# A conditioned transformer block on one core: gate rows in four column groups, order rules for 13 of 64 attention steps, and MLP differences behind the split of the maxima

## Chip, cores and metric

The kernel runs on one core of a Trainium2 chip. The metric is device time in microseconds (us), the median of several executions. One execution was also taken with the hardware profiler.

## What is computed

x is (8, 1024, 512) float32, the condition is (8, 512), with 16 heads of width 32 and an MLP of width 2048. The reference, cut to what matters:

```python
mod = silu(condition) @ Wada + bada
sh_a, sc_a, gt_a, sh_m, sc_m, gt_m = split(mod, 6, axis=1)
xm = layernorm(x, g1, be1) * (1 + sc_a[:, None]) + sh_a[:, None]
x = x + gt_a[:, None] * (causal_attention(xm, Wqkv) @ Wproj + bproj)
xm = layernorm(x, g2, be2) * (1 + sc_m[:, None]) + sh_m[:, None]
h = gelu(xm @ W1 + b1)            # the exact form
x = x + gt_m[:, None] * (h @ W2 + b2)
```

## The kernel before

The 8 x 1024 rows are 16 blocks n of 512 rows: batch n // 2, half h = n % 2. A block of the second half attends to both halves of its batch. Its 16 heads are four groups g of four heads. An attention step is a pair (n, g); there are 64.

**Attention, twice over.** First come the scores of a group (`scores_at_once`, tiles sc_n_g_..., L1791): query tokens by keys, for four heads at once by four row groups of 32. VectorE adds the mask on the diagonal (L1805) and takes row maxima (L1808). `split_maxima` writes each maximum as a sum of three bfloat16 numbers into the tile mcols by four small operations (L1827 to L1830), on GpSimd or VectorE. TensorE turns them into a row (L1846), ScalarE copies that to mrow (L1852). Then `weights_T` computes the transposed scores (tiles st_n_g_k): TensorE first writes the negative maxima (L1872) and then adds the scores (L1884), ScalarE takes the exponent into a tile pT (L1897), GpSimd masks the diagonal (L1902) and sums the tiles pT (L2010). `weigh` multiplies with the values (tile po, L1925), `finish` sums over keys by a matmul with ones (L1946) and normalizes. The tiles sc and st share one place in PSUM, four banks large; po has one; three single banks serve all else.

**Linear work.** All projections and the MLP go through `strassen` and `down`, seven half-size products in place of eight; every product is 16 or 64 matmuls with 128 contraction rows, 32 output rows and 256 columns (`matmul`, L233), four beside each other in four column groups. Products A11 and A12 of a step go into one bank; A12 may start only when the copy p1 of A11 (p_proj for the output projection, L214) is out. In `down`, the second MLP matrix, VectorE and GpSimd make differences of hidden tiles hT (`combine`, L1378) between the products: after the product B22 of part 1 and its sum v3, VectorE replaces B22 by B22 − B12, and two more combinations follow. `settle` multiplies a result by its gate row and adds it to the residual rows xr. Weights arrive through a ring of nine tiles w_0, w_1, ... filled by SyncE's queue.

**Turned rows.** For most blocks the normalized rows are transposed by VectorE in 32 x 32 squares (L817), written to DRAM in four pieces (L830) and read back in four pieces (L836) to become xm_a or xm_m, the input of the projections and of the MLP.

**What sets the order.** While it writes the program, the kernel keeps its own estimate of each engine's time (`now`, `note`, `note_pe`). Linear work runs in threads; `step_aside`, ahead of every attention piece, lets linear work go first until its planned share is done or until the attention piece would wait less than the linear work. Small elementwise operations go through `either`, which takes VectorE only if it would end 1000 ns (`margin`) earlier than GpSimd. Transfers wait in a list (`transfers`) until the queue has room.

**Gate rows.** `gates(kind)` multiplies the activated condition (condT, 8 columns of a 32-column group) with the two gate parts of Wada: for each of four contraction tiles and two halves one matmul of 8 output rows and 256 columns (L582). VectorE adds bada (L222), and for the attention's gate also multiplies bproj by it (L591). The rows of 8 batches go to DRAM in one write each (L596), and `gate_broadcasts` reads one of them into 128 partitions per batch (L602).

## Time and profile before

| | us |
|---|---|
| median of 3 runs | 3461.78 |
| lowest and highest | 3461.54 and 3462.37 |
| the profiled execution | 3463.39 |
| its span | 3461.7 |

| engine | busy us | share | instructions |
|---|---|---|---|
| TensorE matmuls (PE) | 3420.8 | 99% | 55538 |
| weight loads (PEld) | 1775.8 | 51% | 55538 |
| VectorE (DVE) | 2068.1 | 60% | 2304 |
| ScalarE (ACT) | 1289.5 | 37% | 1424 |
| GpSimd (POOL) | 1939.0 | 56% | 2092 |

The granted clock of TensorE is 1.00 in the whole span. In the rows of the profile a line such as L233 is a line of the kernel before; "out<-in" are the tiles written and read, without their numbers, then the shape and the count. A row of the timeline begins with its start and its length in us; what stands in square brackets is idle time of that engine just before and what ended it. A float32 matmul of the program is two instructions in the trace, and matmuls that run beside each other overlap, so busy times of single matmuls don't add up.

### The profile page before, as it was taken

The numbers are of one execution on the slowest core, as the hardware profiler recorded it, in microseconds if no ns is written. First come the engines' busy times: TensorE is split into PE (matmuls) and PEld (weight loads), VectorE is DVE, ScalarE is ACT, GpSimd is POOL, SyncE is SP. The second block draws the span as 40 slices with busy tenths as digits, with TensorE's granted clock in tenths as the row PEclk, the third lists the DMA queues.
The fourth block names the chain that finished last, engine by engine and source line by source line (L and its number), as shares of the span: only waits on it lengthen the run. The fifth ranks groups of instructions, "written<-read, shape, count | busy, mean of one in ns | idle before, by whom it ended". The sixth has DMA issues, their size and how long they took to land.

```text
span 3461.7 us, 122760 instructions
## 1 busy us (share of the span) xinstructions
PE 3420.8 (99%) x55538; PEld 1775.8 (51%) x55538; DVE 2068.1 (60%) x2304; ACT 1289.5 (37%) x1424; POOL 1939.0 (56%) x2092
## 2 busy tenths in 40 slices
PE   8999999999999999999999999999999999999999
PEld 5544554455544554455554455454554545545555
DVE  6765666646566465664657546575466755556454
ACT  2345244343243433434333352433524334242431
POOL 3666757756267472774626755277553775446520
PEclk9999999999999999999999999999999999999999
DMA  7832434345544455444544445444464444633344
GB/s 230 277 124 87 122 113 130 103 126 150 172 136 129 128 151 159 135 139 130 162 145 136 136 133 169 138 134 136 132 177 134 130 146 122 192 110 102 117 144 136
DMA packets 380429, 490.71 MB, mean 142 GB/s; under 512 B 28436, under 2 KB 236364, under 8 KB 379908
## 3 DMA queue, kind: packets, MB, share of 16 engines
q1 hardware_dynamic: 379712, 482.59, 46.4%
q8 instruction: 437, 7.16, 0.8%
q14 instruction: 84, 0.69, 0.1%
q10 hardware_dynamic: 196, 0.28, 0.0%
HBM read 429.22 MB, written 53.53 MB: 139 GB/s over the span
## 4 chain that ended last, share of the span: by engine, by line
PE 89%; DVE 4%; DMA 3%; ACT 2%; issue 1%; POOL 1%; SPq 0%; DVEq 0%; ACTq 0%; POOLq 0%
PE bank L233 61%; PE sc L1791 8%; PE po L1925 7%; PE st L1884 7%; PE st L1872 3%; DVE mx L1808 2%; PE bank L1946 2%; DMA w<-kept_up_S 1%; ACT pT L1897 1%; DMA xm_m<-turned_m 1%; DVE sc L1805 1%; PE bank L1846 1%; DVE hT L1378 0%; ACT hT L1309 0%; PE bank L887 0%
## 5 line engine op out<-in xcount | busy, mean ns | idle before, releaser
L2010 POOL TENSOR_TENSOR pT<-pT,pT 128x256 f32<-128x256 f32 (+3 forms) x1254 | 1218.8, 1007 | 159.6 <-ACT pT L1897 121.9
L1897 ACT ACTIVATE pT<-st 128x2048 f32<-128x2048 f32 x288 | 541.1, 1879 | 1007.8 <-PE st L1884 892.6
L233 PE MATMUL bank<-w,hT 128*32 128x256 f32 x14336 | 814.4, 380 | 0.0
L1808 DVE TENSOR_REDUCE mx<-sc 128x4 f32<-128x2048 f32 (+3 forms) x384 | 665.5, 1754 | 196.3 <-PE sc L1791 190.2
L233 PEld LDWEIGHTS bank<-w,hT 128*32 128x32 f32 x14336 | 453.8, 110 | 357.8 <-issue 74.2
L233 PE MATMUL bank<-xm_m,w 128*32 128x256 f32 x8192 | 499.2, 380 | 1.5 <-issue 1.0
L233 PE MATMUL bank<-t_m,w 128*32 128x256 f32 x6144 | 383.8, 380 | 0.8 <-DMA w<-kept_up_S 0.4
L1902 POOL TENSOR_SCALAR_AFFINE_SELECT pT<-pT 128x512 f32<-128x512 f32 x256 | 181.0, 725 | 359.0 <-ACT pT L1897 357.3
L233 PEld LDWEIGHTS bank<-xm_m,w 128*32 128x32 f32 x8192 | 255.5, 110 | 229.9 <-issue 64.3
L1791 PE MATMUL sc<-kT,qT 32*128 32x512 f32 (+3 forms) x3072 | 329.1, 520 | 3.2 <-DVE mx L1808 3.0
L1805 DVE TENSOR_TENSOR sc<-sc,mask 128x1024 f32<-128x1024 f32 (+1 forms) x160 | 162.7, 1017 | 250.5 <-PE sc L1791 174.0
L1925 PE MATMUL po<-pT,v 128*32 128x512 f32 (+3 forms) x3072 | 304.8, 491 | 0.0
L1884 PE MATMUL st<-qT,kT 32*128 32x512 f32 (+3 forms) x3072 | 300.0, 486 | 0.0
L233 PEld LDWEIGHTS bank<-t_m,w 128*32 128x32 f32 x6144 | 189.9, 110 | 177.3 <-issue 53.1
L233 PE MATMUL bank<-xm_a,w 128*32 128x256 f32 x3968 | 239.5, 380 | 1.8 <-ACT xm_a L902 1.1
L190 POOL TENSOR_TENSOR qT<-top,rec 128x512 f32<-128x512 f32 x59 | 77.3, 1310 | 280.5 <-ACT rec L1964 277.5
L222 DVE TENSOR_TENSOR hT<-bank,u_u 128x512 f32<-128x512 f32 x192 | 130.1, 686 | 150.4 <-PE bank L233 147.4
L1791 PEld LDWEIGHTS sc<-kT,qT 32*128 32x128 f32 x3072 | 129.4, 183 | 159.7 <-issue 58.0
L233 PE MATMUL bank<-w,qT 128*32 128x256 f32 (+1 forms) x3008 | 188.9, 389 | 2.3 <-DVE p_proj L214 2.3
L233 PE MATMUL bank<-t_a,w 128*32 128x256 f32 x2944 | 179.4, 380 | 0.0
L233 PEld LDWEIGHTS bank<-xm_a,w 128*32 128x32 f32 x3968 | 126.7, 110 | 98.0 <-issue 16.1
L1309 ACT ACTIVATE hT<-hT,cols 128x512 f32<-128x512 f32 x256 | 164.1, 711 | 23.1 <-DVE hT L222 22.4
(246 smaller groups left out, 3414.8 us busy)
## 6 DMA issues: line engine op xcount, KB each, us to landing
w<-in_L_cond_W_dram SPq DMA_DIRECT2D x384, 256.0 KB
w<-kept_up_S SPq DMA_DIRECT2D x256, 256.0 KB
w<-kept_down_S SPq DMA_DIRECT2D x256, 256.0 KB
w<-kept_qkv_S SPq DMA_DIRECT2D x180, 256.0 KB
w<-in_L_cond_Wqkv_dram SPq DMA_DIRECT2D x147, 256.0 KB
hat<-in_x_dram SPq DMA_DIRECT2D x64, 256.0 KB
xr<-in_x_dram SPq DMA_DIRECT2D x64, 256.0 KB
out_dram<-xr SPq DMA_DIRECT2D x64, 256.0 KB
```

The source lines that it names most:

```text
L222: nc.vector.tensor_tensor(out, src, other, op)
L233: nc.tensor.matmul(ps[r], columns, rhs, start=start, stop=stop, skip_group_check=True)
L1309: nc.scalar.activation(hT[:, i, :], hT[:, i, :], AF.Gelu, bias=cols[:, O_B1 + f : O_B1 + f + 1])
L1791: nc.tensor.matmul(sc[:, j, c0 : c0 + w], qTs[n][r, gg, ts(qt, P)], keys_of(n, kh)[r, gg, :w], start=True, stop=True, skip_group_check=True,)
L1805: nc.vector.tensor_tensor(place, place, shape_of.to_broadcast(place.shape), ALU.add)
L1808: nc.vector.tensor_reduce(maxima[n, gg][:, kh, qt, :], sc[:, :, c0 : c0 + w], axis=AX.X, op=ALU.max)
L1872: nc.tensor.matmul(st[:, j, c0 : c0 + w], minus_ones[r, :], row[r, TB - w :], start=(c0 == 0), stop=False, skip_group_check=True,)
L1884: nc.tensor.matmul(st[:, j, c0 : c0 + w], kT[r, gg, ts(k % NTT, P)], qT[r, gg, TB - w :], start=False, stop=True, skip_group_check=True,)
L1897: nc.scalar.activation(pT[:, :, :used], st[:, :, :used], AF.Exp, scale=scale)
L1902: nc.gpsimd.affine_select(diagonal, diagonal, pattern=[[0, HPG], [1, P]], compare_op=ALU.is_ge, fill=0.0, base=0, channel_multiplier=-1,)
L1925: nc.tensor.matmul(po[r, TB - w :], v[:, k % NTT, g * P + j * hd : g * P + (j + 1) * hd], pT[:, j, c0 : c0 + w], start=(k == 0), stop=last ...
L2010: nc.gpsimd.tensor_tensor(into, into, pT[:, j, c0 : c0 + w], ALU.add)
```

## The change

**Gates.** Each contraction tile now meets four column groups of 128 columns, with all 32 columns of condT, so that the four quarters of a gate row stand below each other in one bank. The bias rows bada and bproj are loaded as one row each and spread over the groups by a matmul with ones. VectorE copies the result and, for the attention, multiplies the spread bproj by it. Each row then goes to DRAM in four writes of 8 x 128, which wait in the list of transfers.

**Order rules.** A table MANNER gives 13 attention steps their own `margin` and a value `leaning`, all others (1000, 0). A leaning of 300 lets an attention piece go first although linear work could start up to 200 ns earlier, or although it waits 300 ns itself. In `settle`, block 0 has margin 0.

**Behind the split.** After v3, VectorE makes a copy of one column of mcols, if the split in progress is about to end; the MLP differences stand behind that copy in VectorE's queue.

```diff
-    def either(out, a, b, op, reads, writes):
+    def either(out, a, b, op, reads, writes, slack=None):
...
-        if max(now["DVE"], t) + on_dve + margin[0] < max(now["POOL"], t) + on_pool:
+        if max(now["DVE"], t) + on_dve + (margin[0] if slack is None else slack) < max(now["POOL"], t) + on_pool:
...
-    costs = {"at": 16 * TR, "mt": 16 * TR, "gates": 4 * MM, "mod": 4 * MM}
+    costs = {"at": 16 * TR, "mt": 16 * TR, "gates": 2 * MM, "mod": 4 * MM}
...
-        ps = banks[bank][:B, :]
-        for fh in range(2):
-            for k in range(NC):
-                if fh + k:
-                    yield [], []
+        def spread_rows(r, start, stop):
+            for j in range(HPG):
                 nc.tensor.matmul(
-                    ps[:, half(fh, HB)], condT[:, k, :B], part[k // 2, fh][:, k % 2, :],
-                    start=fh + k == 0, stop=k == NC - 1, skip_group_check=True,
+                    banks[bank][j * hd : (j + 1) * hd, ts(r, P)], ones[:1, :hd], rows[r][:, ts(j, P)],
+                    start=start, stop=stop, skip_group_check=True,
                 )
-                note_pe(2 * COLUMN * HB, "columns", [], [("l", bank)])
-        release(*at)
-        combine_out(b_gate, bank, ps, b_gate)
+            note_pe(2 * COLUMN * P, "columns", [], [("l", bank)])
+        for k in range(NC):
+            for j in range(HPG):
+                nc.tensor.matmul(
+                    banks[bank][j * hd : (j + 1) * hd, :P], condT[:, k, :],
+                    part[k // 2, j // 2][:, k % 2, ts(j % 2, P)],
+                    start=k == 0, stop=False, skip_group_check=True,
+                )
+            note_pe(2 * COLUMN * P, "columns", [], [("l", bank)])
+            yield [], []
+        release(*at)
+        for r in range(len(rows)):
+            spread_rows(r, r > 0, True)
+        made = tmp.tile([P, TB], F32, tag="y", name=f"gates_{kind}")
+        gate = made[:, :P]
+        nc.vector.tensor_copy(gate, banks[bank][:, :P])
...
+                    nc.sync.dma_start(there[:, ts(j, P)], made[j * hd : j * hd + B, ts(r, P)])
...
+    def behind_split():
+        if rows_due and now["DVE"] < due([("rows", *rows_due[-1])]) < now["DVE"] + 2500:
+            seen = small.tile([P, 1], BF16, tag="seen", name=f"seen_{rows_due[-1][0]}_{rows_due[-1][1]}")
+            nc.vector.tensor_copy(seen, mcols[:, NTT - 1, 2:3])
+            note("DVE", 60, [("rows", *rows_due[-1])], [])
...
     def settle(n, f, t, y, ky):
...
+        slack = 0 if n == 0 else None
+        add_to(y, gate, [("row", "gm")], [ky], ALU.mult, slack)
+        add_to(residual[n][:, half(t, 2), c], y, [ky], keys, slack=slack)
...
             combine_out(got["v3"], bank, ps, got["u5"], [key("u5")], [key("v3")])
+            behind_split()
             combine(nc.vector, "B22", "B22", "B12")
...
             if done_linear[0] < stream["due"]:
-                if other > own + 100:
+                if other > own + 100 - leaning[0]:
                     break
-            elif own <= max(other, 50):
+            elif own <= max(other, 50) + leaning[0]:
                 break
...
+    MANNER = {(0, 1): (1000, 300), (0, 3): (1000, 300), (1, 3): (-1000, 0), (2, 0): (-1000, 0), (2, 1): (2500, 0), (3, 1): (0, 0), (4, 0): (1000, 300), (6, 0): (1000, 300), (8, 0): (1000, 300), (10, 0): (1000, 300), (12, 1): (2500, 0), (14, 3): (0, 0), (3, 3): (2500, 300)}
...
+                margin[0], leaning[0] = MANNER.get((n, g), (1000, 0))
```

The order of the instructions that follows, at three places. Lines of the kernel after are some 20 to 40 higher than before; a count at a row's end is that of equal instructions, and a trailing number is a tile's own.

VectorE in step (8, 2), where the sum v3 of block 6 is made; mx and sc are maxima and scores of (8, 3), hT_6 are hidden tiles. Before:

```order
L1805 TENSOR_TENSOR sc_8_3_2_0_19958<-sc_8_3_2_0_19958,mask_149 128x4x256
L1808 TENSOR_REDUCE mx_8_3_19588<-sc_8_3_2_0_19958 128x4 x2
L222 TENSOR_TENSOR v3_d_6_19997<-bank_1_96,p5_d_6_19862 128x512
L1378 TENSOR_TENSOR hT_6_2_18716<-hT_6_2_18716,hT_6_0_18291 128x4x256
L1378 TENSOR_TENSOR hT_6_3_18939<-hT_6_3_18939,hT_6_1_18503 128x4x256
```

After, from v3 on:

```order
L222 TENSOR_TENSOR v3_d_6_20031<-bank_0_95,p5_d_6_19891 128x512
L1363 COPY seen_8_3_20033<-mcols_162 128x1
L1408 TENSOR_TENSOR hT_6_2_18746<-hT_6_2_18746,hT_6_0_18333 128x4x256
L1408 TENSOR_TENSOR hT_6_3_18990<-hT_6_3_18990,hT_6_1_18545 128x4x256
L187 TENSOR_TENSOR hT_6_0_18333<-hT_6_2_18746,hT_6_0_18333 128x4x256
L187 TENSOR_TENSOR hT_6_1_18545<-hT_6_3_18990,hT_6_1_18545 128x4x256
L839 STREAM_TRANSPOSE xm_m7_20155<-xh_m7_20073 128x16x32 x4
L222 TENSOR_TENSOR y11_d_6_20210<-bank_2_97,p1_d_6_19747 128x512
```

The copy seen stands ahead of the differences. On TensorE the maxima's row (L1846) stood 8 matmuls of w_629 behind st_8_2_1; now it stands directly behind it.

TensorE in step (8, 0): the output projection of block 7 (w_609 is A11, w_611 is S2, w_610 is A12) around the scores sc_8_2_3. Before:

```order
L233 MATMUL bank_1_96<-w_609_19186,qT_7_15399 32x256 x4
L233 MATMUL bank_0_95<-w_611_19227,t2_7_19350 32x256 x16
L233 MATMUL bank_1_96<-w_610_19205,qT_7_15399 32x256 x4
L1791 MATMUL sc_8_2_3_0_19450<-kT_8_18068,qT_8_17893 128x512 x4
L233 MATMUL bank_1_96<-w_610_19205,qT_7_15399 32x256 x12
L233 MATMUL bank_2_97<-w_612_19267,qT_7_15399 32x256 x16
```

After:

```order
L1962 MATMUL po_8_0_19402<-pT_8_0_1_19077,v_8_19248 32x128 x4
L233 MATMUL bank_1_96<-w_609_19225,qT_7_15444 32x256 x8
L233 MATMUL bank_0_95<-w_611_19266,t2_7_19389 32x256 x16
L1828 MATMUL sc_8_2_3_0_19485<-kT_8_18068,qT_8_17927 128x512 x4
L233 MATMUL bank_1_96<-w_610_19244,qT_7_15444 32x256 x16
L233 MATMUL bank_2_97<-w_612_19306,qT_7_15444 32x256 x16
```

All of A12 now stands behind the scores.

SyncE's queue around step (6, 3): xm_m5 is the MLP input of block 5, xr_4 the finished rows of block 4. Before:

```order
L1353 DMA out_0_dram<-xr_4_11471 4x32x512
L391 DMA w_489_15499<-in_L0_cond_Wqkv_dram 128x2x256
L391 DMA w_490_15518<-in_L0_cond_W1_dram 128x2x256
L1353 DMA out_0_dram<-xr_4_11471 4x32x512
L391 DMA w_491_15538<-in_L0_cond_W1_dram 128x2x256
L1353 DMA out_0_dram<-xr_4_11471 4x32x512 x2
L836 DMA xm_m5_15077<-turned_m5_15079 128x512 x4
```

After:

```order
L1383 DMA out_0_dram<-xr_4_11511 4x32x512
L393 DMA w_485_15462<-kept_qkv_1_S2_271 128x512
L858 DMA xm_m5_15137<-turned_m5_15139 128x512 x2
L393 DMA w_486_15502<-kept_qkv_1_S1_268 128x512
L393 DMA w_487_15504<-kept_qkv_1_S3_286 128x512
L393 DMA w_488_15523<-kept_qkv_1_S4_289 128x512
L858 DMA xm_m5_15137<-turned_m5_15139 128x512
L391 DMA w_489_15545<-in_L0_cond_Wqkv_dram 128x2x256
L391 DMA w_490_15566<-in_L0_cond_W1_dram 128x2x256
L858 DMA xm_m5_15137<-turned_m5_15139 128x512
L391 DMA w_491_15586<-in_L0_cond_W1_dram 128x2x256
L1383 DMA out_0_dram<-xr_4_11511 4x32x512 x3
```

The four reads of xm_m5 now stand ahead of three of the four stores. On VectorE their four transposes stand together; before, 14 rows of other work stood between the first and the other three.

41 lines of the change are left out of this document (25 added, 16 removed).

## The prediction

> **What bounds the kernel.** I read the page first: busy time, then the chain that ended last; then TensorE's busy time in three stretches, the waits of TensorE, and the timeline at the places where it waits.
>
> ```profile
> PE 3420.8 (99%) x55538; PEld 1775.8 (51%) x55538; DVE 2068.1 (60%) x2304; ACT 1289.5 (37%) x1424; POOL 1939.0 (56%) x2092
> PE 89%; DVE 4%; DMA 3%; ACT 2%; issue 1%; POOL 1%; SPq 0%; DVEq 0%; ACTq 0%; POOLq 0%
> 0.00:100.00 100.00, 85.74 (x1348) 50.97 (x1348) 65.01 (x98) 31.54 (x44) 39.38 (x58) 1.00 0.68 226
> 100.00:3400.00 3300.00, 3277.39 (x53130) 1690.33 (x53134) 1977.19 (x2174) 1254.09 (x1374) 1895.79 (x2032) 1.00 0.47 139
> 852.09 45.32 PE bank L233 x840
> ```
>
> TensorE is busy 99% of the span, at granted clock 1.00 (the last column but two of the stretches). It can gain only by less matmul work, fewer changes between its forms, or shorter waits. Of waits, 3300 − 3277.4 = 22.6 us lie between 100 and 3400 us; the first 100 us hold 14.3 more, mostly before the first product. The chain's longest quiet piece gives the price of linear work: 45.32 / 840 = 0.054 us for each pass of 256 columns. A float32 matmul shows as two passes, so one matmul of the program is 0.108 us.
>
> Where TensorE waits (engine and line, what it waited for, us in total, times, longest):
>
> ```profile
> PE st L1872 <- DVE mx L1808: 8.1, 13, 1.9
> PE bank L1846 <- POOL mcols L1830: 5.9, 7, 1.6
> PE bank L233 <- DVE p_proj L214: 2.3, 5, 0.5
> ```
>
> These understate a little. A wait is counted from the modelled end of the matmul before, and that end overhangs: below, 16 passes are given as 1.07 us though 16 x 0.054 = 0.86. So 0.1 to 0.2 us more was lost at each. I price waits by the starts.
>
> **The gates.** The matmuls now have 128 columns in four column groups instead of 256 columns with 8 output rows.
>
> ```profile
> 104.47 1.04 PE L523 MATMUL bank<-w,condT 128*32 128x128 f32 x16
> 105.44 0.40 PE L1872 MATMUL st<-mrow,minus_ones 32*128 32x384 bf16 x8
> 149.72 1.46 PE L582 MATMUL bank<-w,condT 128*8 128x256 f32 x6
> 151.11 1.14 PE L1791 MATMUL sc<-kT,qT 32*128 32x512 f32 x8
> ```
>
> Old price: 1.39 us from start to start for 6 passes, less 0.11 for the change of form, is 0.213 each; 32 passes make 6.8 us. New shape: the modulation (L523) has it already, 16 passes in 0.97 − 0.11 = 0.86 us, so 0.054 each. That is no cheaper than 256 columns. After the change there are 32 matmuls of the gates and 12 that spread the bias rows, 88 passes, 4.75 us. **Saved: 2.1 us.** If 128 columns took half of 0.054, it would be 4.4.
>
> The page "TensorEngine Tiling (Array Packing)" of the Trainium skill, "Theoretical Speedup", gives up to 4 times for an output dimension of at most 32. By that estimate the 6.8 us would become 1.7 and the spreading little more, some 2 us better than my sum. The L523 row speaks against that: 4 groups of half the width gained nothing over 0.054.
>
> Twelve small writes replace three on SyncE's queue; at 0.3 us of issue each that is 2.9 us more of the queue within 70 us. The ring of nine weight tiles covers it; without that cover it costs at most 2.9.
>
> **The split of the maxima.** GpSimd splits the row maxima in four small operations (L1827 to L1830) while VectorE makes the MLP differences (L1378).
>
> ```profile
> 843.45 0.41 PE L1846 MATMUL bank<-ident_b,mcols 128*32 128x128 bf16 x16 [1.60 <-POOL mcols L1830]
> 1693.10 0.26 POOL L1827 CAST mcols<-mx 128x16 bf16<-128x16 f32 x1 [1.78 <-DVE mx L1808]
> 1693.55 2.35 DVE L1378 TENSOR_TENSOR hT<-hT,hT 128x1024 f32<-128x1024 f32 x2
> 1693.73 1.15 POOL L1829 CAST mcols<-rest 128x16 bf16<-128x16 f32 x1
> 1694.49 1.07 PE L233 MATMUL bank<-w,hT 128*32 128x256 f32 x16
> 1694.96 1.07 POOL L1830 TENSOR_TENSOR mcols<-rest,mcols 128x16 bf16<-128x16 f32 x1
> 1696.08 0.41 PE L1846 MATMUL bank<-ident_b,mcols 128*32 128x128 bf16 x16 [0.52 <-POOL mcols L1830]
> 1671.69 0.25 POOL L1827 CAST mcols<-mx 128x16 bf16<-128x16 f32 x1 [3.55 <-DVE mx L1808]
> 1672.65 0.27 POOL L1830 TENSOR_TENSOR mcols<-rest,mcols 128x16 bf16<-128x16 f32 x1
> ```
>
> Alone the split takes 1.23 us (1671.69 to 1672.92); here 2.93, since two of its operations stretch from 0.25 to over 1 us as L1378 begins. TensorE's own work ended at 1694.49 + 0.86 = 1695.35, so it lost 0.73 us. With the differences held back the split ends at about 1694.33, when TensorE still computes st: no wait. The same happens in (4,2), (10,2), (12,2) and (14,2), the last cured by a new order. That is four of 0.73 and, at 843.45, one of 1.3 to 1.6: **4.2 us.** Behind the waiting copy stand four difference operations, four transposes and the sum y11. All come about 1 us later. TensorE works meanwhile on product B21, 64 matmuls or 6.9 us, and has two other banks, so I cost this at nothing; uncovered it is 5 x 1 us.
>
> **Transposes in time.** In (6,3) the transposed rows of the MLP's input came late.
>
> ```profile
> 1274.26 0.70 DVE L817 STREAM_TRANSPOSE xm_m<-xh_m 128x512 f32<-128x512 f32 x1
> 1290.29 1.89 DVE L817 STREAM_TRANSPOSE xm_m<-xh_m 128x512 f32<-128x512 f32 x3
> 1309.14 1.48 SPq L1353 DMA_DIRECT2D out_dram<-xr  x2
> 1310.67 4.32 SPq L836 DMA_DIRECT2D xm_m<-turned_m  x4
> 1322.78 0.64 PE L233 MATMUL bank<-xm_m,w 128*32 128x256 f32 x8 [1.01 <-issue]
> 1323.79 1.50 PE L233 MATMUL bank<-xm_m,w 128*32 128x256 f32 x24 [0.37 <-DVE xm_m L896]
> 1327.31 1.14 PE L1791 MATMUL sc<-kT,qT 32*128 32x512 f32 x8 [2.02 <-DVE mx L1808]
> ```
>
> Three transposes stood behind 16 us of other work, so the four reads back (L836) went behind the stores and their data arrived as TensorE needed it: waits of 1.01, 0.37 and 2.02, by starts 3.8 us. In the new order all four transposes stand together and the reads stand ahead of three stores. **Saved: 3.8 us.**
>
> **Order rules.** Two repeated waits, in block 8:
>
> ```profile
> 1646.38 0.64 PE L233 MATMUL bank<-w,qT 128*32 128x256 f32 x8 [0.38 <-DVE p_proj L214]
> 1664.50 1.15 PE L1791 MATMUL sc<-kT,qT 32*128 32x256 f32 x16
> 1664.71 4.51 DVE L1378 TENSOR_TENSOR hT<-hT 128x1024 f32<-128x1024 f32 x2
> 1665.58 6.68 PE L233 MATMUL bank<-w,hT 128*32 128x256 f32 x120
> 1669.15 1.22 DVE L1805 TENSOR_TENSOR sc<-sc,mask 128x1024 f32<-128x1024 f32 x1
> 1672.81 0.40 PE L1872 MATMUL st<-mrow,minus_ones 32*128 32x384 bf16 x8 [0.55 <-DVE mx L1808]
> ```
>
> First, w_610 waits for the copy p_proj out of its bank. The new order puts scores (1.08 us with the change of form) ahead of it, so the wait goes, as do those of (4,0) and (10,0). The list has five, 2.3 us or 0.63 each by starts; three make 1.9 us. Second, the scores' mask stands behind 4.51 us of differences. Now the scores stand 36 matmuls (3.9 us) further ahead of st_8_1_1; in (12,1) the rule changes instead which engine adds. Three waits of 0.65: 2.0 us. Three single waits get work put before them in the same way, 1.8 us in the rows and 2.0 by starts:
>
> ```profile
> 444.59 0.64 PE L233 MATMUL bank<-xm_a,w 128*32 128x256 f32 x8 [0.70 <-ACT p_k L217]
> 2891.09 0.40 PE L1872 MATMUL st<-mrow,minus_ones 32*128 32x384 bf16 x8 [0.66 <-DVE mx L1808]
> 2936.76 1.15 PE L1791 MATMUL sc<-kT,qT 32*128 32x256 f32 x16 [0.42 <-DVE mx L1808]
> ```
>
> Block 0's last sums move to VectorE by the rule of no margin, three operations; nothing in the list of waits stands there, so I cost them at nothing, at most 3 x 0.6 us (half of an L1378 operation each).
>
> Against these: the first attention steps.
>
> ```profile
> 115.81 0.40 PE L1872 MATMUL st<-mrow,minus_ones 32*128 32x512 bf16 x4 [1.87 <-DVE mx L1808]
> ```
>
> Here ten more matmuls (1.1 us) now lie between the scores and the next use of their tile, so I take 1.0 off. In (0,3) the order leaves less work there, 0.75 back, and in blocks 1's first two steps three places lose 0.3 to 0.6, together 1.0 back. TensorE changes form 1183 times instead of 1188; one costs 0.11 into the row form and 0.21 after scores (1665.58 − 1664.50 − 0.86): 0.7 us less.
>
> **Waits that the order doesn't show.** TensorE's order changes in 50 of 64 steps. The old order waited 22.6 us between 100 and 3400 us, some 27 by starts, most of it in those steps; new places will wait too. Bounds: none, and 15 us, as much as was removed. I take 2.5, near the lower end, as the counted stretches between users of the score tile show few new shortages above 0.3 us.
>
> **Sum:** −2.1 − 4.2 − 3.8 − 1.9 − 2.0 − 2.0 − 1.0 + 0.75 + 1.0 − 0.7 + 2.5 = −13.5, taken as −13. The profiled execution took 3463.4 us for a span of 3461.7; the median of the runs shown is 3461.8, 1.6 below it. From the median: **3449 us.**
>
> **Rivals.**
> - *New waits replace the old ones.* 50 re-ordered steps with 0.2 us more each would give 10 us back: 3459. Against it: the repeated waits are removed by 1 to 4 us of room, not by a hair. Chance 0.15.
> - *The attention leans too far (slower).* Seven steps may start a score or weight tile though it waits 0.3 us longer. They hold about 40 such tiles. If each waits the 0.3 and as much again where VectorE is late, 40 x 0.6 = 24 us come and 13 go: 3473. It decides from 0.3 us a tile on. For it: masks that stretch as at 1669.15. Against it: by the order only some ten tiles there fall short, mostly by 0.02. Chance 0.06.
> - *The lock moves on.* A GpSimd operation beside VectorE's differences is stretched; held back 1 us, these may stretch the next one instead:
>
> ```profile
> 1648.19 1.22 POOL L1902 TENSOR_SCALAR_AFFINE_SELECT pT<-pT 128x512 f32<-128x512 f32 x2
> 1696.65 2.48 POOL L1902 TENSOR_SCALAR_AFFINE_SELECT pT<-pT 128x512 f32<-128x512 f32 x2 [0.63 <-ACT pT L1897]
> ```
>
>   Two selects cost 1.26 us more there than alone. If TensorE pays that in all five places, 6.3 of the 13 are lost: 3455. Against it: the weights of these tiles are used later than the split. Chance 0.05. The page "SBUF — State Buffer" of the Trainium skill, "Who interferes with whom", says that GpSimd and such a VectorE operation share a port pair, and that the second to issue fully blocks until the first finishes. The rows agree; by that rule, holding VectorE back only chooses the victim.
> - *The rules move nothing that matters.* Only the gates count: 3459 to 3460. Chance 0.02; the rows of the order speak against it.
>
> **How the numbers follow.** The forecast, 3443 to 3454, has 0.72. The range of 8 in 10 reaches to 3459 for the first rival and down to 3442 for half-price gates and no new waits. Within 0.2% (6.9 us) is about what a measurement of this kernel can tell from no change. Faster by more: 0.72 + 0.04 of the cases near 3455 = 0.76; within: 0.17; slower: 0.07.
>
> **What would show it.** The gates' matmuls at 0.054 us a pass; no wait of L1846 (now L1883) for GpSimd past 100 us; splits of 1.2 us; no wait at 1322 us; p_proj's waits down from five to two; TensorE idle between 100 and 3400 us near 12 us. I am wrong if that idle time stays at 20, or if new lines lead the list of waits.

## The result and the profile after

The changed kernel takes **3445.49 us** (median of 6 runs, 3443.98 to 3452.48) against 3461.66 for the kernel before (median of 6, 3458.48 to 3469.83): a ratio of 0.9954, 95% interval [0.9941, 0.9967]. The forecast was 3449, with a range of 3442 to 3459. The profiled execution has a span of 3442.9 us, 18.8 less than the one before; the medians differ by 16.2.

The page gives TensorE's busy time of the changed kernel:

```profile
PE 3414.4 (99%) x55594; PEld 1772.7 (51%) x55594; DVE 2070.1 (60%) x2317; ACT 1283.6 (37%) x1418; POOL 1920.2 (56%) x2088
```

The view by windows of the changed kernel has the same two stretches as were read before (after the stretch's length come TensorE's busy time, that of its weight loads, VectorE, ScalarE and GpSimd, the granted clock, the DMA share and GB/s):

```profile
0.00:100.00 100.00, 87.31 (x1430) 53.01 (x1434) 65.53 (x102) 31.67 (x44) 39.47 (x58) 1.00 0.72 240
100.00:3400.00 3300.00, 3288.24 (x53454) 1696.52 (x53450) 1985.08 (x2191) 1251.35 (x1373) 1876.86 (x2028) 1.00 0.47 140
```

TensorE is idle for 3300 − 3288.2 = 11.8 us between 100 and 3400 us, where it was 22.6. That is "near 12", as forecast. The list of TensorE's waits in the changed kernel (us in total, times, longest):

```profile
PE st L1909 <- DVE mx L1845: 5.1, 12, 1.4
PE bank L1883 <- POOL mcols L1867: 3.2, 4, 1.6
PE sc L1828 <- DVE mx L1845: 1.1, 2, 0.7
```

L1909, L1883 and L1828 are the old L1872, L1846 and L1791; their waits were 8.1, 5.9 and 3.0. No wait for p_proj is left at all; five stood there. Of the four waits for the split of the maxima, two lie before 100 us (1.61 and 0.64), one of 0.27 stands in step (2,0), and one of 0.71 in (14,2), which should have gone, is still there.

Here is the new form of the gates, from the timeline of TensorE in the changed kernel (start, length, line, operation, and count of passes):

```profile
86.33 1.06 PE L589 MATMUL bank<-w,condT 128*32 128x128 f32 x32
87.32 0.42 PE L581 MATMUL bank<-b_ga,ones 1*32 1x128 f32 x8
87.56 0.40 PE L581 MATMUL bank<-b_gba,ones 1*32 1x128 f32 x8
```

From start to start 32 passes take 0.99 us, so **0.031 us a pass** (0.030 for the 8 passes of the first bias row), not the 0.054 that the prediction had taken from the modulation. The 88 passes of the gates cost about 2.7 us, where the old 32 passes cost 6.8.

And this is the split in (8,2), from the timeline of the changed kernel, with the waiting copy of VectorE (L1363):

```profile
1680.61 0.26 POOL L1864 CAST mcols<-mx 128x16 bf16<-128x16 f32 x1 [1.72 <-DVE offset_m L729]
1680.97 1.09 PE L1921 MATMUL st<-qT,kT 32*128 32x384 f32 x16
1681.24 0.26 POOL L1866 CAST mcols<-rest 128x16 bf16<-128x16 f32 x1
1681.58 0.27 POOL L1867 TENSOR_TENSOR mcols<-rest,mcols 128x16 bf16<-128x16 f32 x1
1681.88 0.16 DVE L1363 COPY seen<-mcols 128x1 bf16<-128x1 bf16 x1 [0.66 <-POOL mcols L1867]
1681.95 2.35 DVE L1408 TENSOR_TENSOR hT<-hT,hT 128x1024 f32<-128x1024 f32 x2
1681.99 0.41 PE L1883 MATMUL bank<-ident_b,mcols 128*32 128x128 bf16 x16
```

The four operations take 1.24 us (1680.61 to 1681.85) and end while TensorE still computes st, which ends near 1681.99; the matmuls of L1883 follow without a wait.

### The profile page after: what moved, and what is told of

It is laid out like the page before. It is cut to its first block, busy times and chain, and to the rows that moved or that the text cites. A ratio compares the mean times of both kernels' runs of the same rounds, so it can differ in the third digit from the quotient of the medians.

```text
span 3442.9 us, 122860 instructions
## 1 busy us (share of the span) xinstructions
PE 3414.4 (99%) x55594; PEld 1772.7 (51%) x55594; DVE 2070.1 (60%) x2317; ACT 1283.6 (37%) x1418; POOL 1920.2 (56%) x2088
## 4 chain that ended last, share of the span: by engine, by line
PE 92%; ACT 3%; DVE 3%; DMA 1%; issue 1%; POOL 1%; SPq 0%; DVEq 0%; ACTq 0%; POOLq 0%
PE bank L233 64%; PE sc L1828 9%; PE po L1962 7%; PE st L1921 7%; PE st L1909 3%; PE bank L1983 2%; DVE mx L1845 1%; ACT pT L1934 1%; ACT hT L1331 1%; PE bank L1883 0%; DMA xm_m<-turned_m 0%; DVE sc L1842 0%; ACT L1331 0%; PE bank L909 0%; ACT L170 0%
## 5 line engine op out<-in xcount | busy, mean ns | idle before, releaser
L233 PE MATMUL bank<-w,hT 128*32 128x256 f32 x14336 | 812.9, 380 | 0.0
L233 PEld LDWEIGHTS bank<-w,hT 128*32 128x32 f32 x14336 | 454.3, 110 | 357.0 <-issue 72.3
L233 PE MATMUL bank<-xm_m,w 128*32 128x256 f32 x8192 | 500.2, 380 | 0.8 <-ACT p_u L217 0.8
L233 PE MATMUL bank<-t_m,w 128*32 128x256 f32 x6144 | 381.2, 380 | 0.2
L233 PEld LDWEIGHTS bank<-xm_m,w 128*32 128x32 f32 x8192 | 255.0, 110 | 229.2 <-issue 65.4
L1939 POOL TENSOR_SCALAR_AFFINE_SELECT pT<-pT 128x512 f32<-128x512 f32 x256 | 172.2, 691 | 351.4 <-ACT pT L1934 349.9
L1828 PE MATMUL sc<-kT,qT 32*128 32x512 f32 (+3 forms) x3072 | 329.1, 520 | 1.3 <-DVE mx L1845 1.1
L233 PEld LDWEIGHTS bank<-t_m,w 128*32 128x32 f32 x6144 | 189.8, 110 | 174.7 <-issue 45.6
L233 PE MATMUL bank<-xm_a,w 128*32 128x256 f32 x3968 | 238.8, 380 | 1.7 <-ACT xm_a L924 1.1
L1828 PEld LDWEIGHTS sc<-kT,qT 32*128 32x128 f32 x3072 | 129.4, 183 | 159.6 <-issue 59.2
L233 PE MATMUL bank<-w,qT 128*32 128x256 f32 (+1 forms) x3008 | 187.7, 389 | 0.0
L233 PE MATMUL bank<-t_a,w 128*32 128x256 f32 x2944 | 178.8, 380 | 0.5 <-DVE qT L222 0.5
L233 PEld LDWEIGHTS bank<-xm_a,w 128*32 128x32 f32 x3968 | 126.4, 110 | 100.6 <-issue 18.6
```

What stands on the lines that cost most here:

```text
L233: nc.tensor.matmul(ps[r], columns, rhs, start=start, stop=stop, skip_group_check=True)
L1828: nc.tensor.matmul(sc[:, j, c0 : c0 + w], qTs[n][r, gg, ts(qt, P)], keys_of(n, kh)[r, gg, :w], start=True, stop=True, skip_group_check=True,)
L1939: nc.gpsimd.affine_select(diagonal, diagonal, pattern=[[0, HPG], [1, P]], compare_op=ALU.is_ge, fill=0.0, base=0, channel_multiplier=-1,)
```

## The experiments

The theory that went into them: the gain is the sum of separate cures, the gates about 4 us, the split about 4, the waits that the order rules remove about 6, and the transposes in (6,3) 3.8. The first rival: each edit shifts the planner's clock, the program re-plans what follows, and a new order brings as many waits as it takes, so that no edit has a worth of its own.

### Each edit alone, and the changed kernel without one

**The gates alone** (the changed kernel without the call of the split's copy, without the line that reads MANNER, and with the usual margin in block 0):

```diff
-            behind_split()
-        slack = 0 if n == 0 else None
+        slack = None
-                margin[0], leaning[0] = MANNER.get((n, g), (1000, 0))
```

> The kernel before with the new form of the gates alone: no behind_split, no MANNER, no slack for block 0's sums. Because the gates' products come sooner to an end in the planner's clock and their pieces are fewer, 40 of 64 steps of TensorE's order change by this edit alone, the step (6,3) among them, which gets the order that it has in the changed kernel. Theory A (the form saves what the changed kernel's rows show, 6.8 - 88 x 0.031 = 4.1 us, and the four transposes in (6,3) now stand together, 3.8 us): span 8 us under that of before, about 3453.5, and no wait before L233 on xm_m at about 1320 us. Rival B (a new order is worth nothing on the whole, as many waits come as go): 4.1 us, about 3457.5. The splits of the maxima still wait in blocks 8, 10 and 12 (0.5 us each in the list of waits).

Measured: 3462.02 us, ratio 1.0003 [0.9994, 1.0012]. Nothing is gained, so both theories fall short. The waits of the step (6,3) at 1322 are gone as expected, though TensorE now waits 0.94 us there for a weight tile, at 1328.10. But the new order brings a wait in (2,0) that neither kernel had in this length. The timeline of this kernel, TensorE and VectorE:

```profile
385.58 1.14 PE L1827 MATMUL sc<-kT,qT 32*128 32x512 f32 x8
385.64 1.49 DVE L187 TENSOR_TENSOR y_d<-y_d,row_gm 128x512 f32<-128x512 f32 x1
387.17 1.63 DVE L187 TENSOR_TENSOR xr<-xr,y_d 128x512 f32<-128x512 f32 x1
388.73 0.69 DVE L1841 TENSOR_TENSOR sc<-sc,mask 128x512 f32<-128x512 f32 x1
389.45 2.29 DVE L1844 TENSOR_REDUCE mx<-sc 128x4 f32<-128x2048 f32 x1
391.80 0.61 PE L1908 MATMUL st<-mrow,minus_ones 32*128 32x512 bf16 x4 [5.08 <-DVE mx L1844]
392.20 1.92 PE L1920 MATMUL st<-qT,kT 32*128 32x512 f32 x8
```

No linear work is left between the scores and st, two sums of block 0 stand ahead of the mask on VectorE, and TensorE waits 5.08 us. What follows is worth as much: L1920 takes 1.92 us, where the same eight passes take 1.02 elsewhere. The windows of this kernel around that place:

```profile
380.00:389.60 9.60, 6.72 (x108) 2.90 (x100) 4.58 (x5) 2.46 (x2) 9.36 (x8) 0.98 0.40 138
389.60:396.00 6.40, 4.21 (x30) 1.67 (x32) 2.14 (x1) 1.73 (x1) 6.40 (x10) 0.50 0.22 82
396.00:405.00 9.00, 9.00 (x152) 4.77 (x152) 4.26 (x4) 3.17 (x6) 3.48 (x8) 0.99 0.20 60
```

In the middle stretch the granted clock is 0.50; in finer slices it falls at 389.3, while TensorE still waits, and comes back at 396.1, 6.8 us later. TensorE is busy for 4.21 us of the stretch, so the halved clock costs 2.1 us on top of the wait of 5.1. A wait of 2.31 us that ends at 113.02 goes with 3.4 us at half clock (112.8 to 116.2) in the same way. Together these take back the 4.2 us of the gates (measured by themselves below) and the 3.8 of (6,3).

**The split alone** (the kernel before with behind_split and its call):

```diff
+            behind_split()
             combine(nc.vector, "B22", "B22", "B12")
```

> The kernel before with behind_split alone; 8 of 64 steps change their order. Theory A: the splits in (4,2), (8,2), (10,2), (12,2), (14,2) take 1.2 us instead of 2.9 and TensorE does not wait there: 4.2 us less, about 3457.5. Rival (the lock moves on to GpSimd's next operation and TensorE pays there): 3460 to 3462.

Measured: 3456.29 us, ratio 0.9984 [0.9976, 0.9993], so 5.3 us less. From the shift of TensorE's starts against the kernel before, 1.68 us come in (4,2) and about 0.73 in each of the four others, 4.6 us in all. Theory A holds. (Two waits that have nothing to do with the split are gone as well, 1.32 us at 1106.21 and 1.02 at 1957.20 in the kernel before; more of them below.) GpSimd's next operations, the two selects, are stretched to 2.21 us in (8,2), as the rival says, but TensorE does not wait for them.

**The rules alone** (the kernel before with MANNER, `leaning` and the line that reads them):

```diff
+                margin[0], leaning[0] = MANNER.get((n, g), (1000, 0))
                 if (n, g) == groups[-1]:
```

> The kernel before with MANNER and the leaning alone; 37 of 64 steps change their order, (6,3) again into that of the changed kernel. Theory A (the waits that the prediction gave to the rules: p_proj 1.9, masks behind differences 2.0, single waits 2.0, the first steps 1.0 - 0.75 - 1.0, and the transposes of (6,3) 3.8): 9 us less, about 3453. Rival B (the rules move nothing that matters): within 2 us of before. Rival C (seven steps lean too far): slower than before.

Measured: 3469.35 us, ratio 1.0017 [1.0008, 1.0026], so **slower than before** by 7.8 us. Theory A missed by 16 us, with the sign wrong. The list of waits of this kernel shows one part:

```profile
PE bank L1849 <- POOL mcols L1833: 10.0, 9, 1.6
PE bank L233 <- DVE p_proj L214: 4.7, 1, 4.7
```

The waits for the split grew from 5.9 to 10.0: in the new order the maxima's rows stand closer behind st, so a split that is stretched is waited for 1.6 us where it was 0.5. The second row is one event, which the timeline of this kernel shows:

```profile
3121.43 5.61 DVE L187 TENSOR_TENSOR qT<-t,qT 128x512 f32<-128x512 f32 x1 [4.16 <-POOL pT L2013]
3122.54 1.23 POOL L1905 TENSOR_SCALAR_AFFINE_SELECT pT<-pT 128x512 f32<-128x512 f32 x2
3123.73 2.76 POOL L2013 TENSOR_TENSOR pT<-pT,pT 128x256 f32<-128x256 f32 x4
3126.96 0.68 DVE L214 COPY p_proj<-bank 128x512 f32<-128x512 f32 x1
3127.69 1.08 PE L233 MATMUL bank<-w,qT 128*32 128x256 f32 x8 [4.68 <-DVE p_proj L214]
```

One VectorE operation on 512 columns takes 5.61 us while GpSimd works through its pT operations (the two of that size in the run of the gates alone took 1.5 and 1.6). The copy that TensorE needs stands behind it. Again the clock is halved, from shortly before the wait ends (windows of this kernel):

```profile
3120.00:3126.90 6.90, 3.02 (x56) 1.52 (x48) 5.47 (x1) 1.88 (x1) 6.49 (x11) 0.99 0.24 77
3126.90:3133.30 6.40, 5.61 (x43) 1.92 (x47) 3.72 (x4) 0.00 (x0) 0.00 (x0) 0.50 0.01 3
```

That is 4.7 us of waiting and 2.8 us (half of 5.61) of slow work from one neighbourhood of two engines. Four of the eleven executions took 3463.9 to 3466.0 us and seven 3468.5 to 3471.0, which fits an event that comes in some executions only; only one of the seven was profiled, so this is not shown.

**The changed kernel without the rules:**

```diff
-                margin[0], leaning[0] = MANNER.get((n, g), (1000, 0))
```

> The changed kernel without MANNER and the leaning (the line that reads MANNER is left out); 36 of 64 steps have another order than in the changed kernel. Theory A (the rules bring 1.9 + 2.0 + 2.0 + 0.25 on top of the rest; the step (6,3) keeps its new order): about 5 to 6 us over the changed kernel, 3450 to 3452. Rival B (the gates and the split do it all): within 1.5 us of the changed kernel.

Measured: 3458.2 us, ratio 0.999 [0.9981, 0.9999], 12.7 us over the changed kernel: twice what theory A gave, and rival B falls. The wait of (0,2) is back with 2.31 us at 112.60; (2,0) waits 2.65 at 390.80, where the gates alone waited 5.08; and new ones are 1.58 in (1,0) at 218.67 and 1.45 at 172.56 on GpSimd. The clock is halved for 3.4 us each from 220.2 and from 390.8, which costs 3.3 of the 12.7 us.

**The changed kernel without the split:**

```diff
-            behind_split()
```

> The changed kernel without the call of behind_split: five copies on VectorE less, and but for one step, (12,2), TensorE's order is that of the changed kernel. Theory A (the split is stretched by the differences to 2.9 us and TensorE waits for it, 0.73 in four steps and 1.3 to 1.6 in one): 4.2 us over the changed kernel, about 3447 of span against 3442.9. Rival (the lock only moves on to the select of pT): under 1.5 us over it.

Measured: 3455.13 us, ratio 0.9982 [0.9973, 0.9991], so 9.6 us over the changed kernel by the medians (11.1 if each is compared with the kernel before on its own chip). But for one step TensorE's order is the same, so the two traces can be laid beside each other: TensorE falls behind by 1.68 us in each of (4,2), (6,2), (8,2) and (10,2), and by 0.73 in (12,2), 7.4 us in all. In (6,2) the kernel before had no such wait. A further 1.6 us come at 216 us, where the clock is halved in this profile and not in that of the changed kernel. The same place in (8,2), from the timeline of this kernel:

```profile
1687.28 2.35 DVE L1408 TENSOR_TENSOR hT<-hT,hT 128x1024 f32<-128x1024 f32 x2
1687.39 1.22 POOL L1865 CAST mcols<-rest 128x16 bf16<-128x16 f32 x1
1688.69 1.07 POOL L1866 TENSOR_TENSOR mcols<-rest,mcols 128x16 bf16<-128x16 f32 x1
1689.81 0.41 PE L1882 MATMUL bank<-ident_b,mcols 128*32 128x128 bf16 x16 [1.60 <-POOL mcols L1866]
```

As VectorE's differences begin, two GpSimd operations stretch from 0.26 to over 1 us, and TensorE waits 1.60. So theory A's mechanism holds, and its size is that of the old order: in the new one the copy is worth 7.4 us and not 4.6.

**Split and rules with the old gates** completes the eight combinations:

```diff
-    costs = {"at": 16 * TR, "mt": 16 * TR, "gates": 2 * MM, "mod": 4 * MM}
+    costs = {"at": 16 * TR, "mt": 16 * TR, "gates": 4 * MM, "mod": 4 * MM}
...
+        combine_out(b_gate, bank, ps, b_gate)
```

> The kernel before with behind_split, MANNER, the leaning and block 0's slack, but the old gates, noted as in the kernel before: 39 of 64 steps differ from before, 29 from the changed kernel. It completes the eight combinations of the three edits. Theory A (MANNER was fitted to the order that the gates and the split give; in another order it leaves or makes waits as it does in the run with MANNER alone): the split's five waits of 1.6 us go, so about 8 us under the run with MANNER alone, 3460 to 3462, with the wait for p_proj at about 3123 us and a halved clock behind it still there. Rival B (the edits add up): before - 5.3 of the split + 7.8 of the rules, about 3464. Rival C (the split and the rules are what matters, the gates only their 4.5): about 3450.

Measured: 3453.68 us, ratio 0.9979 [0.997, 0.9988], between the expectations. The five waits for the split are gone, as theory A said, but the long wait for p_proj did not come back, although the same operations stand there in the same order. The same VectorE operation in the timeline of this kernel, again in the midst of GpSimd's pT operations (L2024 from 3106.87 to 3112.87):

```profile
3111.27 0.87 DVE L187 TENSOR_TENSOR qT<-t,qT 128x512 f32<-128x512 f32 x1 [4.16 <-POOL pT L2024]
```

It takes 0.87 us and not 5.61. So the 7.5 us in the run of the rules alone did not follow from the order of the queues by itself. All the combinations, in us against the kernel before on the same chip:

| gates | split | rules | median, us | before, us | difference |
|---|---|---|---|---|---|
| new | – | – | 3462.02 | 3461.58 | +0.4 |
| – | yes | – | 3456.29 | 3461.58 | −5.3 |
| – | – | yes | 3469.35 | 3461.58 | +7.8 |
| new | yes | – | 3458.20 | 3461.58 | −3.4 |
| new | – | yes | 3455.13 | 3460.25 | −5.1 |
| – | yes | yes | 3453.68 | 3461.78 | −8.1 |
| new | yes | yes | 3445.49 | 3461.66 | −16.2 |

(The rows with two edits also hold block 0's rule of no margin, those with one do not.) The three edits alone add up to +2.9 us; together they bring −16.2. The rules are worth +7.8 alone (with the one event of 7.5 in it), −2.8 on top of the split, −5.5 on top of the gates and −12.8 on top of both. So the first rival is right about any part, and wrong about the whole: these rules have their worth only in the order that they were set for.

### The gates' form by itself

The old products were put in the place of the new ones, with the planner's costs, pieces and transfers as in the changed kernel, so that TensorE's order is the same elsewhere; the bias rows are added on VectorE, not by TensorE:

```diff
-                    banks[bank][j * hd : (j + 1) * hd, :P], condT[:, k, :],
-                    part[k // 2, j // 2][:, k % 2, ts(j % 2, P)],
+                ps[:, half(fh, HB)], condT[:, k, :B], part[k // 2, fh][:, k % 2, :],
...
+            if fk % 2:
+                note_pe(2 * COLUMN * P, "columns", [], [("l", bank)])
```

> The changed kernel with the gates' products in the old form (256 columns, 8 output rows, one column group; the bias rows are added on VectorE and not by TensorE), with the notes for the planner, the pieces and the transfers as in the changed kernel, so that TensorE's order is the same everywhere else. By the changed kernel's rows (0.031 us a pass, 88 passes, against 32 passes at 0.213): 4.1 us over it. By the prediction's 0.054 a pass: 2.1 us over it.

Measured: 3447.99 us (3447.60 to 3448.91), ratio 0.9963 [0.9949, 0.9976], 2.5 us over the changed kernel by the medians and 3.3 by the profiled spans. The intervals of the two kernels overlap, so the rows have to decide. TensorE's timeline in this kernel:

```profile
86.74 3.62 PE L582 MATMUL bank<-w,condT 128*8 128x256 f32 x16
90.29 0.40 PE L1900 MATMUL st<-mrow,minus_ones 32*128 32x512 bf16 x4
```

3.55 us from start to start for one set of gates, where the new form takes 1.61 (86.33 to 87.94). That is 1.94 us. Over the second set and its bias row the shift of TensorE's starts grows from 2.34 to 4.56 us, by 2.22, so 4.2 us of TensorE's time in all, as the 0.031 foretold. Of these 0.75 are given back at once: in the changed kernel TensorE waits 0.68 for the maxima at 158.12, and in this one, which comes later, it does not. The rest of the way to 3.3 are small waits that differ between the two profiles in spite of the same order, 1.26 us more in (5,2) and 1.8 less in three places after it.

Why did the modulation pay 0.054 for the same shape? In its loops two matmuls to two column groups follow each other, then the next contraction tile's to the same two groups; the gates' loops go through all four. The changed kernel with the modulation's loops turned round:

```diff
-        for fh in range(2):
-            for k in range(NC):
+        for k in range(NC):
+            for fh in range(2):
                 for jj in range(2):
```

> The changed kernel with the modulation's products in another order of their loops: the four column groups in succession instead of two and two; nothing else moves. Theory A (a pass costs 0.054 with two column groups beside each other and 0.031 with four): the 64 passes past 100 us cost 1.5 us less, L523 shows 0.032 us a pass, and the 64 passes in the first 16 us may bring as much again unless the loads set the pace there: 1.5 to 2.9 us under the changed kernel. Rival (the gates' low price has another cause, such as their place or their start flags): L523 stays at 0.054 a pass and the time is the same.

Measured: 3443.95 us (3443.18 to 3451.53), ratio 0.9955 [0.9943, 0.9968], not to be told from the changed kernel. But the rows tell. TensorE's timeline of the changed kernel, then of this one:

```profile
109.76 1.06 PE L523 MATMUL bank<-w,condT 128*32 128x128 f32 x20
111.82 0.40 PE L1909 MATMUL st<-mrow,minus_ones 32*128 32x512 bf16 x4 [1.00 <-DVE mx L1845]
```

```profile
109.95 0.84 PE L523 MATMUL bank<-w,condT 128*32 128x128 f32 x20
112.01 0.40 PE L1909 MATMUL st<-mrow,minus_ones 32*128 32x512 bf16 x4 [1.22 <-DVE mx L1845]
```

The 20 passes got shorter by 0.22 us, and the wait for VectorE behind them longer by 0.22. Nothing was gained there, and as little at 140 us. Only the two pieces of 12 passes brought something, 0.4 us in all; from start to start they take 0.54 us for 0.76, and less the 0.11 of the change of form that is 0.036 a pass for 0.054. In the first 16 us nothing was gained either: the first product of L233 starts at 17.61 in both kernels. So theory A is right that the succession of column groups sets the price, since nothing else was moved, but the four pieces got shorter by 0.9 us and not by 1.5, and it is wrong on the time: the places have another bound.

### Other doubts of the prediction

**The delay of the differences,** costed at nothing because product B21 covers it. Eight copies in the place of one:

```diff
+            for _ in range(8):
-            nc.vector.tensor_copy(seen, mcols[:, NTT - 1, 2:3])
+                nc.vector.tensor_copy(seen, mcols[:, NTT - 1, 2:3])
```

> The changed kernel with eight copies of the split's last column on VectorE instead of one, so that the MLP differences behind them start about 1 us later in five places; TensorE's order is the same. Theory A (product B21, 6.9 us of TensorE, covers the delay): within 0.5 us of the changed kernel. Rival (VectorE is the next bound there, the lock or the delay is handed on): up to 5 us over it.

Measured: 3445.82 us (3443.81 to 3446.66), ratio 0.9954 [0.9942, 0.9967], the same as the changed kernel. The timeline in (8,2) of this kernel:

```profile
1683.86 1.49 DVE L1364 COPY seen<-mcols 128x1 bf16<-128x1 bf16 x8 [0.66 <-POOL mcols L1868]
1685.06 5.35 PE L233 MATMUL bank<-w,hT 128*32 128x256 f32 x96
```

The differences start 1.3 us later, and TensorE runs through its 96 passes; in none of the five places do its starts shift. The delay is covered, as was taken.

**The leaning without the margins:**

```diff
-                margin[0], leaning[0] = MANNER.get((n, g), (1000, 0))
+                leaning[0] = MANNER.get((n, g), (1000, 0))[1]
```

> The changed kernel with the second numbers of MANNER (the leaning) alone and all margins at 1000; 13 of 64 steps differ from the changed kernel, those from (1,3) to (3,2) and (12,1), (14,3) to (15,2). Theory A (the leaning cures the long waits at 112 and 386 us, the margins the wait of the masks in (12,1) and small ones in blocks 1 to 3): 2 to 4 us over the changed kernel. Rival B (the margins only move small work): within 1 us of it. Rival C (without the margins a wait comes back in blocks 1 to 3 that halves the clock): 5 us or more over it.

Measured: 3449.59 us, ratio 0.9966 [0.9952, 0.9979], 4.1 us over the changed kernel by the medians, with overlapping intervals. The long waits of (0,2) and (2,0) stay cured, that of 0.70 us on p_k at 442.98 comes back and so do 0.51 and 0.58 in (12,1): this fits theory A, at its upper end.

**The halved clock.** Delays of growing length on VectorE were to make TensorE wait:

```diff
+    PROBE = {(5, 1): 12, (7, 1): 20, (9, 1): 28, (11, 1): 36, (13, 1): 48}
...
+        for _ in range(PROBE.pop((n, g), 0)):
+            held = small.tile([P, 1], F32, tag="held", name=f"held_{n}")
+            nc.vector.tensor_copy(held, b2_rows[:, 0, :1])
```

> The changed kernel with 12, 20, 28, 36 and 48 small copies on VectorE (about 0.18 us each, 2.2 to 8.9 us) ahead of the first row maxima of the steps (5,1), (7,1), (9,1), (11,1) and (13,1), so that TensorE waits there, each time longer; its order is the same. Theory A (a wait of some 2 us or more within a few us makes the chip grant TensorE half its clock for 3 to 7 us afterwards): behind the longer of the five waits the clock shows 0.50 and the products run at half speed, 1.6 to 3.4 us lost for each on top of the wait; behind a wait under 1.5 us nothing. Rival (the halved clock in other runs fell there by chance): the clock stays at 1.00 behind all five, and the time grows by the waits alone.

Measured: 3447.26 us (3445.78 to 3453.44), ratio 0.9962 [0.9949, 0.9974]. The question was not put: the copies took 0.095 us each, not 0.18, and the longest group ended like this (timeline of this kernel):

```profile
2621.74 4.54 DVE L1847 COPY held<-b_rows 128x1 f32<-128x1 f32 x48
2626.20 2.28 DVE L1849 TENSOR_REDUCE mx<-sc 128x4 f32<-128x2048 f32 x1
2628.54 1.14 PE L1829 MATMUL sc<-kT,qT 32*128 32x512 f32 x8 [0.87 <-DVE mx L1849]
```

4.54 us of extra VectorE work cost TensorE 0.87, and the clock stayed at 1.00. What the run does show is the cover: the 36 copies in (11,1), 3.4 us, cost TensorE nothing.

**A further version.** (14,2) still has a stretched split in the changed kernel, since other differences (L187, of operand B21) begin there. The modulation's turned loops and one more waiting copy ahead of these:

```diff
+            if n == 12:
+                behind_split()
             combine(nc.gpsimd, "B21", "B21", "B22")
```

> The changed kernel with the modulation's four column groups in succession and one more call of behind_split, ahead of the differences B21 of block 12's MLP, where the split in (14,2) is still stretched; but for these TensorE's order is that of the changed kernel. Theory A: no wait of L1883 for GpSimd at about 2959 us, 0.7 less, and 0.4 less from the modulation (two of its gains became waits for the maxima): 1.1 us under the changed kernel, 3444.4, and less than the measurement can tell. Rival (the held-back differences B21 are needed sooner than the v3 ones): a wait of as much behind them, 3445.5 or more.

Measured: 3444.43 us (3443.72 to 3447.36), ratio 0.9954 [0.9941, 0.9966], not to be told from the changed kernel, as theory A says. The cure itself works. The timeline in (14,2) of the changed kernel, then of this one:

```profile
2956.48 2.35 DVE L187 TENSOR_TENSOR hT<-hT 128x1024 f32<-128x1024 f32 x2
2957.89 1.07 POOL L1867 TENSOR_TENSOR mcols<-rest,mcols 128x16 bf16<-128x16 f32 x1
2959.01 0.41 PE L1883 MATMUL bank<-ident_b,mcols 128*32 128x128 bf16 x16 [0.71 <-POOL mcols L1867]
```

```profile
2960.49 0.27 POOL L1869 TENSOR_TENSOR mcols<-rest,mcols 128x16 bf16<-128x16 f32 x1
2961.79 0.41 PE L1885 MATMUL bank<-ident_b,mcols 128*32 128x128 bf16 x16
```

The wait of 0.71 us is gone, and TensorE's starts gain 0.78 there.

## Why the prediction held, and where its steps failed

**What bounds the kernel** was read rightly: TensorE's idle time between 100 and 3400 us went from 22.6 to 11.8 us. Over the whole span, by the two pages, it fell by 12.4 us and TensorE's busy time by 6.4; these make the 18.8.

**The gates** were mis-sized: 2.1 us forecast, 4.2 measured in the same order. The step that failed is the comparator. The L523 row had the shape, 128 columns in 32-column groups, but not the succession of groups, and the modulation with turned loops shows that this sets the price. The estimate of up to 4 times from the page "TensorEngine Tiling (Array Packing)" of the Trainium skill, "Theoretical Speedup", which the prediction held the row against, was nearer: the 64 passes of the products cost 2.0 us for the old 6.8, where it gives 1.7.

**The split** came to 4.6 us alone, for a forecast of 4.2 (3.9 without the place in (14,2)). "The last cured by a new order" was wrong: (14,2) still waits 0.71. In the changed kernel the copy prevents 7.4 us, since the new order would have exposed the split more: 1.68 us in each of (4,2), (6,2), (8,2) and (10,2), where the order before lost 1.68 in (4,2), 0.73 in (8,2) and (10,2), and nothing in (6,2). **Its cover** held.

**The transposes of (6,3)** went as forecast: the waits at 1322 are gone, and only one of 0.2 stands near (1300.19). But the prediction named no edit for it, and it needs neither the split nor the rules: the new gates alone re-plan the step so, and the rules alone do too.

**The order rules:** the three masks in (8,1), (10,1), (12,1) and the three single waits are gone. Of p_proj's waits five went and not three; those in later blocks vanish by re-planning, 1.2 us more than forecast. In block 0 the wait in (0,2) fell from 1.87 to 1.00, and that in (0,3) grew by 0.8 (by starts) for a forecast of 0.75.

**Waits that the order doesn't show,** taken at 2.5 us, came to more: the list of single waits of the changed kernel has 4.2 us in thirteen places that the sum doesn't name, 0.2 to 0.7 each. The largest wait at a new place is 0.77 at 266.03 on p_u, in block 1's second step, for which the sum had allowed.

**Waits that the sum forgot.** The kernel before has three long waits that no term of the prediction names: 1.32 us at 1106.21 in (5,2), 1.02 at 1957.20 in (9,2) and 0.97 at 3291.10. All three are gone in the changed kernel, 3.3 us. The first, from the timeline of the kernel before, and then VectorE's same operation in that of the changed kernel:

```profile
1099.89 1.63 DVE L896 TENSOR_SCALAR xm_m<-xm_m,gainm,shiftm 128x512 f32<-128x512 f32 x1 [0.78 <-DMA xm_m<-turned_m]
1106.21 0.40 PE L1872 MATMUL st<-mrow,minus_ones 32*128 32x512 bf16 x4 [1.32 <-DVE mx L1808]
```

```profile
1093.20 0.55 DVE L918 TENSOR_SCALAR xm_m<-xm_m,gainm,shiftm 128x512 f32<-128x512 f32 x1 [0.75 <-DMA xm_m<-turned_m]
```

The operation starts when its piece of xm_m has landed. In the kernel before it runs beside GpSimd's sums of pT, from 1099.96 on, and takes three times as long; in the changed kernel it is over before they begin (at 1094.07). This too is not in the order of the instructions: the kernel with the gates' old form, whose order there is that of the changed kernel, waits 1.02 us at the same place.

So the total came out 3.5 us better than forecast by the medians, 5.3 by the profiled spans. The named causes are the gates (2.1) and p_proj (1.2). The idle time met its forecast of 12 partly by luck: 3.3 us of waits that nobody had priced went away, while the new waits and (14,2) brought back some 2.4 us more than the sum had. What held is the way of summing, over the places of the final order, for the terms it named. Summed over the edits it would have failed: the theory for the experiments did that, and put the rules alone at −9 where they measured +7.8, or about 0 without the one long event. The rival "leans too far" had named slower, but what the profile of the rules alone shows is the exposed splits, one blocked VectorE operation and a halved clock, not the leaning of whole steps. "The lock moves on" was seen: the two selects behind the split take 2.21 us in (8,2), where two alone take 1.22. TensorE does not pay for it.

## What to carry to other kernels

Where a planner sets the order, an edit is worth what the final order makes of it: read the place-by-place order of the whole change, and don't price edits one by one or keep one that was set for another order. Take the price of a small matmul from a row with the same succession of column groups, not only the same shape. A stretched operation that costs half a microsecond in one order can cost three times as much in the next (0.5 us of wait in (8,2) became 1.6), so an order between two engines, here one copy that waits, is a sturdier cure than room. And when an idle time meets its forecast, compare the lists of single waits too: two misses can cancel.

## What the runs showed of the hardware

Float32 matmuls of 128 columns into 32-column groups took 0.031 us a pass with four groups in succession and 0.054 with two and two; one group of 8 rows with 256 columns took 0.22 (3.55 / 16).

The same VectorE operation in the same order took 5.61 us in one kernel and 0.87 in another while GpSimd was busy beside it, and another 1.63 in one and 0.55 in another, so what a blocked operation costs can't be read from the order.

The granted clock fell to 0.50 in several profiles, each time within or behind a wait or a cluster of short waits and nowhere else past 100 us. It stayed down for 6.8 us with the waits of 5.08 and 4.68, and for 3.4 us everywhere else: with single waits of 2.65, 2.31 and 1.58, and in four profiles with four waits of 0.2 to 0.6 at about 215. It isn't certain for a given wait: without the rules the same wait of 2.31 us at 112.60 left the clock at 1.00, the four short waits left it in the changed kernel, and the cluster in (6,3), 1.0 + 0.4 + 2.0 us, left it in the kernel before, while 0.8 + 0.4 + 2.0 halved it in the kernel with the split alone. There, in the timeline of TensorE, scores of 8 passes take 2.09 us for 1.14:

```profile
1324.21 2.09 PE L1799 MATMUL sc<-kT,qT 32*128 32x512 f32 x8 [2.02 <-DVE mx L1816]
```

The page "TensorE: Matmul & The Clock Gate" of the Trainium skill, "Part 1: The HAM clock gate", says that this clock follows TensorE's activity in a free-running window of about 3.4 us. The stretches of 3.4 and 6.8 us, and one wait with and without its halved clock, agree with that. Its rule in "HAM oscillation — how this bites in real kernels", to have no idle gap above some 3.4 us, looks too mild for these traces, where the clock fell with a wait of 2.31 us, and once with one of 1.58.

A wait of two to five microseconds came with about half as much again in slow work (2.1 us on top of 5.1, 2.8 on top of 4.7). The 1.6 us by which profiles of one order differ at 216 come from this. That waits cause it is argued from these places, not shown: the run that was to test this made no wait long enough, and from which length on the clock falls stays open.
